# Self and value weights by two levels of Strassen's algorithm as well, in a two-layer graph network

## The chip, the cores and the metric

The kernel runs on one core of a Trainium2 chip. The metric is the time of one execution on the device, in microseconds. Below, PE or TensorE is the matrix engine, DVE or VectorE, ACT or ScalarE, POOL or GpSimd are the other three that compute, and SP issues DMAs.

## The reference

`x` has 128 graphs of 64 nodes with 768 features, `adj` a 64x64 mask for each; all is float32. Two layers, each with a residual and a layer norm:

```python
# layer 0
p     = softmax(h @ h.T / sqrt(768)) * adjacency
attn  = p / (sum(p) + 1e-10)
ctx   = triu(attn, 1) @ (h @ W_left.T + b_left) + diag(attn) * (h @ W_self.T + b_self) \
      + tril(attn, -1) @ (h @ W_right.T + b_right)
x     = layernorm(x + relu(layernorm(ctx) * gamma + beta))
# layer 1, 12 heads of 64
q, k, v = x @ Wq + bq, x @ Wk + bk, x @ Wv + bv
scores  = q @ k.T / 8 + beta * adj, masked where adj is 0
x       = layernorm(x + softmax(scores) @ v)
```

Six weights of 768x768 are applied to all 8192 rows: left, self and right in layer 0, queries, keys and values in layer 1. Everything else is small beside that.

## The kernel before

The rows are taken in 16 blocks of 512 (four tiles of 128 tokens, eight graphs). The input of a block lies turned in SBUF (`hT` for layer 0, `xT` for layer 1: 128 partitions x 6 chunks x 512 tokens). A weight is streamed from DRAM through the pool `wst` (17 buffers of 128x384) for every block.

**Strassen's algorithm, one level.** Weights and inputs are cut in two by two quarters, and seven products replace eight (the variant of Winograd, which shares sums). The sums of weights are formed once at the start and kept in DRAM. The sums of a block's input are formed by GpSimd (`combined`, `combined4`: S1, S2, S4 and an in-place difference, four operations on 128x768). `seven` runs the seven products in the order `ORDER`; each is three matmuls (three chunks of 128 features) into a PSUM bank, for each of two token halves. The variant accumulates in PSUM, so that a bank is read, written on and read again. VectorE empties a bank with one addition (a bias or a partial result). This is how self (`self_part`), values (`values`), and queries and keys (`projected`) are computed, and in blocks 0 to 2 left and right (`side_part`).

**Two levels.** From block 3 on (`DEEP`), left and right are computed together by `both_sides`: each of the seven products, a 256x384 by 384x384 problem, is cut once more. Of the three feature chunks the first two form a 2x2 problem that again takes seven products, and the third is added plainly, two chunks to a product where it fits: the products numbered 2, 5, 4 and 3 take two matmuls, 1, 6 and 7 take one, 11 matmuls for 12. `second_level` forms the sums of one outer factor on GpSimd (four operations: three of 128x128 and one of 128x256). The function `nested` lays the 49 products out: the inner order is 1, 2, 6, 5, 7, 4, 3, and the next outer sum's products 1 and 2 stand ahead of this one's 4 and 3; the outer order is `ORDER2`, 7, 1, 2, 6, 5, 4, 3. What leaves a bank is added into the result in SBUF, and around outer sum 5 GpSimd has twelve additions of result quarters (four into `c21`, four into `c12`, four into `c22`). Each bank's next product waits until VectorE has emptied it. In `both_sides` the left and the right weight stand side by side, so that a matmul has 2 x 192 = 384 columns. The sums of weights for this are made in blocks 0 and 1 by `deepened`: loads by SP, copies and stores by GpSimd's DMA queue, subtractions by VectorE.

**The order of work.** From the line with `manual_schedule` on, every engine runs its instructions in the order in which the code issues them. Around each block the stages follow each other on TensorE: left and right of block n+1, self of block n+1, values of block n, and three rounds of queries and keys of block n. The rest is hung on places of these stages: `at(hooks, place, f)` calls `f` ahead of the product with that number. Left and right have 28 places (`left` 0 to 13, `right` 0 to 13, spread over the 49 products where there are two levels), `own` (self) and `val` (values) 14 each, and each of `qk[0..2]` 14. Between products, `step` takes pieces of work from three queues, `first`, `urgent` and `lazy`. Such pieces are the turns (`turned`: six transposes of 128x512 on VectorE make `hT` or `xT` from a squared layout), the mask of layer 1 (`mask`), the softmax pieces of `scores`, and layer 1's finish (`finish_by_act`: sums of a tile by ScalarE, `mean` on VectorE, sums of squares by ScalarE, `variance` on VectorE, a root, two factors, the normed tiles, four output DMAs on GpSimd's queue). A `GAP` in a queue lets one step pass. In a light step only pieces that are marked run. `settle(key)` issues at once whatever is left of a key.

`weighted(n, hg)` multiplies the softmax of layer 1 with the values for a third of the heads; VectorE divides (`shares`) and GpSimd adds the shares to the residual.

Of the kernel before, what the change touches and what calls it, by code (L numbers as in the profile page):

```python
# [17 lines left out]
P = 128  # L18
# [27 lines left out]
ORDER2 = (7, 1, 2, 6, 5, 4, 3)  # L46
MATRICES = (1, 2, 8, 3, 9, 5, 7, 4, 6)
DEEP = 3


@with_exitstack
def gnn_two_layers(ctx: ExitStack, tc, x, adj, wl, bl, ws, bs, wr, br, gamma, beta,
# [8 lines left out]
    s_p = ctx.enter_context(tc.tile_pool(name="s_p", bufs=1))  # L61
    s2_p = ctx.enter_context(tc.tile_pool(name="s2", bufs=2))
    l0 = ctx.enter_context(tc.tile_pool(name="l0", bufs=1))
    l0t = ctx.enter_context(tc.tile_pool(name="l0t", bufs=T))
    tmp = ctx.enter_context(tc.tile_pool(name="tmp", bufs=2))
    wst = ctx.enter_context(tc.tile_pool(name="wst", bufs=17))
    st = ctx.enter_context(tc.tile_pool(name="st", bufs=2))
# [194 lines left out]
    def deepened(i):  # L262
# [24 lines left out]
        return begin, [(partial(formed, 0),), (partial(formed, 1),), (end, "gap")]  # L287

    def transposed(src, xT, t):

        both = two_banks("ps_x").rearrange("p b (c i) -> p b c i", c=4)
        for c0 in range(0, KC, 3):
            ps = both[:, c0 // 3]
            for c in range(3):
                nc.tensor.transpose(ps[:, c, :], src[:, c0 + c :: KC], ident)
            nc.scalar.copy(xT[:, c0 : c0 + 3, t * P : (t + 1) * P], ps[:, 0:3, :])
# [23 lines left out]

    def combined(xT, n=None):

        a11, a12 = xT[:, 0:HC, 0:HTOK], xT[:, HC:KC, 0:HTOK]
        a21, a22 = xT[:, 0:HC, HTOK:NTOK], xT[:, HC:KC, HTOK:NTOK]
        s1, s2 = (s_p.tile([P, HC, HTOK], F32, tag=f"S{i}", name=f"S{i}") for i in (1, 2))
        nc.gpsimd.tensor_tensor(s1, a21, a22, ALU.add)
        nc.gpsimd.tensor_tensor(a21, a11, a21, ALU.subtract)
        S = {1: a11, 2: a12, 4: a22, 5: s1, 6: s2, 7: a21}
        if n is not None and n >= DEEP:

            S["deep"] = {i: second_level(S[i]) for i in ORDER2[:2]}
        nc.gpsimd.tensor_tensor(s2, s1, a11, ALU.subtract)
        return S
# [94 lines left out]

    def nested(width, sums, load, multiply, view, C, bias0, bias1, hooks):

# [12 lines left out]
        def taken(i, q, ps, dst, add):  # L443
            if add is None:
                nc.scalar.copy(dst, view(ps))
            else:
                nc.vector.tensor_tensor(dst, view(ps), add, ALU.add)  # L447
# [16 lines left out]
        def sub(i, j):  # L464
            for place in range(28):
                if place * 49 // 28 == len(done):
                    for f in hooks.get(place, ()):
                        f()
# [5 lines left out]
            ps = (X if j in (1, 6, 7, 4) else Y)[i][:, 0:width]  # L474
            multiply(F[i], W[i], j, ps)
            if j == 1:
# [10 lines left out]
            elif j == 3:  # L487
                final(i, (0, 1), ps, U[i, 2])

            step(len(done) > 8, j in (5, 1, 4))  # L490

# [101 lines left out]
    def self_part(n, in_sbuf, hooks={}):  # L593

        blk = blocks[n]
        blk["x_all"] = x1_p.tile([P, T, D], F32, tag="x1", name=f"o_{n}")
        o = [blk["x_all"][:, t, :] for t in range(T)]

        def last(t, h, ps, part):
            cols = slice(h * HALF, (h + 1) * HALF)  # L600
            nc.vector.tensor_tensor(o[t][:, cols], ps, bias["s"][:, cols] if part is None else part, ALU.add)

        by_tokens("s", blk["S"], last, in_sbuf, hooks)
        blk["x"] = o

    def side_part(n, nm, in_sbuf, hooks={}):
# [17 lines left out]
    def both_sides(n, hooks):  # L624
# [15 lines left out]

        def multiply(F, w, j, ps):
            f, last = F
            fs = [(f[j], w[j])]
            if j in (2, 5, 4, 3):
                fs.append((last[{2: 1, 5: 2, 4: 2, 3: 3}[j]], w[8 if j in (2, 4) else 9]))
            for k, (a, b) in enumerate(fs):
                nc.tensor.matmul(ps, lhsT=a, rhs=b, start=(k == 0 and j in (1, 2, 5)), stop=(k == len(fs) - 1),  # L647
                                 skip_group_check=True)

        def view(ps):  # L650
# [3 lines left out]
                       for a in range(2) for b in range(2)} for m in range(2) for n_ in range(2)}  # L654
        nested(HALF, sums, load, multiply, view, C,
               lambda b: bias_lr[:, :, b * QUAD : (b + 1) * QUAD],
# [110 lines left out]
    def values(n, hooks={}, in_place=False):  # L767
# [19 lines left out]

        by_tokens("v", blocks[n]["S"], last, None, hooks)
        if not in_place:
# [80 lines left out]
    def weighted(n, hg, halves=(0, 1)):  # L870
# [6 lines left out]
        eT = blk["eT", hg]  # L877
        y = [two_banks(f"ps_y{r}")[:, 0 : len(halves), 0 : 4 * (HD + 1)]
             .rearrange("p h (t c d) -> p h t c d", t=2, c=2) for r in range(2)]
        for k, h in enumerate(halves):  # L880
# [23 lines left out]
    def finish_by_act(n, tiles=range(T), queue=urgent):  # L904
# [34 lines left out]
        def act(f):  # L939
            return f, "act" if queue is urgent else "root"  # L940

        settle(("y", n, 0))
        settle(("y", n, 1))
        later(key, (partial(sums, lambda t, o: nc.scalar.activation(o, xt[t], AF.Identity,  # L944
                                                                    accum_out=total[:, t : t + 1])), "after"),
              GAP, GAP, tiny(mean),
              act(partial(sums, lambda t, o: nc.scalar.activation(o, xt[t], AF.Square, bias=nm[:, t : t + 1],  # L947
                                                                  accum_out=var[:, t : t + 1]))),
              GAP, GAP, tiny(variance), act(root), GAP, tiny(factors),
              *[act(partial(norm, tiles[k : k + 2])) for k in range(0, len(tiles), 2)],  # L950
# [75 lines left out]
    nc.gpsimd.memset(v[:, :, :, :, HD], 1.0)  # L1026

# [3 lines left out]
    for n in range(NBLK):  # L1033
# [12 lines left out]
        for i, (when, hooks, place) in zip(ORDER2, ((0, val, 2), (0, val, 8), (0, qk[0], 8), (0, qk[1], 6),  # L1046
                                                    (0, qk[2], 6), (1, own, 3), (1, val, 3))):
            if when == n:
                begin, steps = deepened(i)
                at(hooks, place, begin)  # L1050
                at(hooks, place + 3, lambda i=i, steps=steps: urgent.extendleft([(("d", i), *f) for f in reversed(steps)]))

        last = n == NBLK - 1
        if p >= 0:
            one = left if not last else qk[0]
            at(one, 2, scores, p, 2, *((1,) if last else (2, None, 4)))
            at(one, 5, weighted, p, 1)
# [3 lines left out]
            elif not last:  # L1061
                at(right, 1, weighted, p, 2)
                at(right, 2, finish_by_act, p)
            else:
                at(qk[1], 5, weighted, p, 2)

        if not last:
            if n > 0:
# [26 lines left out]

                at(own, 3, turn1)

                def sums1():
                    settle(("t1", n))
                    blocks[n]["S"] = combined(blocks[n]["xT"])  # L1100

# [13 lines left out]
                if m == DEEP:  # L1115
                    settle("d")
                if m < DEEP:
                    side_part(m, "l", None, left)
                    side_part(m, "r", None, right)
                    at(own, 0, lambda: nc.vector.tensor_tensor(bias_lr[:, :, HALF:D], bias_lr[:, :, HALF:D],  # L1120
                                                               bias_lr[:, :, 0:HALF], ALU.subtract))
                else:
                    for t, f in enumerate(both_sides(m, {**left, **{2 * len(ORDER) + k: f for k, f in right.items()}})):
                        at(own, 1 + t, f)
# [85 lines left out]
```

## Time and profile before

| | |
|---|---|
| median of 3 runs | 3017.47 us (3014.36 to 3019.05) |
| the profiled execution | 3019.44 us, its span 3017.7 us |
| granted TensorE clock, mean | 0.988 |
| HBM traffic | 539.43 MB read, 77.27 MB written |

One block from the middle, stage by stage, from the stretches of the trace:

| stage | from - to, us | length | PE | DVE | ACT | POOL |
|---|---|---|---|---|---|---|
| left and right of block 9 | 1599.2 - 1660.1 | 60.9 | 57.0 | 34.4 | 21.7 | 34.4 |
| self of block 9 | 1660.1 - 1687.2 | 27.1 | 27.1 | 17.9 | 10.0 | 5.4 |
| values of block 8 | 1687.2 - 1720.9 | 33.7 | 33.7 | 17.9 | 8.1 | 1.8 |
| queries and keys of block 8 | 1720.9 - 1783.3 | 62.4 | 61.9 | 41.7 | 33.1 | 10.5 |

Busy times of an engine are unions of its instructions' spans. A float32 matmul of the program shows as two instructions on PE, each with a weight load on PEld. A span of PE runs on after the next matmul has begun, so the distance between starts tells the rate. The values stage also holds the 16 matmuls of layer 0's context.

### The profile page before, as it was taken

How to read it: one execution, taken by the hardware profiler on the slowest of the kernel's cores; microseconds unless marked ns; L12 is line 12 of the kernel's file. 1: busy time of each engine (PE TensorE's matmuls, PEld its weight loads, DVE VectorE, ACT ScalarE, POOL GpSimd, SP SyncE). 2: the span in 40 equal slices, each digit the busy share in tenths (PEclk: the TensorE clock that was granted, in tenths of full speed). 3: DMA queues.
4: the chain of work that ended last, by engine and by line, in shares of the span. 5: the costliest groups of instructions: out<-in, count | busy, mean ns of one | idle time of the engine just before them, and what ended most of it. 6: DMA issues, size and time to landing. Idle time of an engine off the chain costs nothing.

```text
span 3017.7 us, 49120 instructions
## 1 busy us (share of the span) xinstructions
PE 2907.4 (96%) x17578; PEld 1941.9 (64%) x17578; DVE 1830.7 (61%) x3151; ACT 1129.4 (37%) x2120; POOL 828.0 (27%) x981
## 2 busy tenths in 40 slices
PE   8999999999999999999999999999999999999996
PEld 5557667575675856657575675756758566585684
DVE  5847666565655656556565565656656565566544
ACT  0104324354243443435334343442435424343354
POOL 3132323314042140512405033050331404214011
PEclk9999999999999999999999999999999999999998
DMA  9677876849577586875958668495774967758442
GB/s 317 212 250 254 243 232 193 241 134 279 153 211 222 151 266 151 228 209 170 255 141 263 168 192 242 134 277 156 205 224 140 278 152 229 203 162 257 135 122 77
DMA packets 440273, 613.14 MB, mean 203 GB/s; under 512 B 53584, under 2 KB 416720, under 8 KB 440032
## 3 DMA queue, kind: packets, MB, share of 16 engines
q1 hardware_dynamic: 362096, 493.57, 54.7%
q10 hardware_dynamic: 60848, 44.05, 7.8%
q0 software_dynamic: 17088, 72.37, 6.8%
q8 instruction: 143, 2.34, 0.3%
q14 instruction: 98, 0.80, 0.1%
HBM read 539.43 MB, written 77.27 MB: 204 GB/s over the span
## 4 chain that ended last, share of the span: by engine, by line
PE 77%; ACT 11%; DVE 5%; DMA 5%; issue 1%; POOL 0%; SPq 0%; ACTq 0%; DVEq 0%
PE ps_X L393 30%; PE ps_Y L393 23%; PE ps_Y L647 9%; PE ps_X L647 8%; ACT eT L858 5%; PE ps_ctx L686 3%; ACT unused L947 2%; PE sc L841 2%; DMA wlr<-lr_d 2%; ACT unused L944 2%; PE u L536 1%; ACT uqk L810 1%; PE ps_y L887 1%; DMA sq<-x1d 1%; ACT L858 1%
## 5 line engine op out<-in xcount | busy, mean ns | idle before, releaser
L900 POOL TENSOR_TENSOR o<-o,shares 128x512 f32<-128x512 f32 (+1 forms) x102 | 126.4, 1248 | 1388.6 <-DVE shares L896 1309.7
L393 PE MATMUL ps_X<-xT,wqk 128*128 128x256 f32 x1728 | 396.9, 381 | 9.1 <-ACT uqk L810 9.1
L393 PEld LDWEIGHTS ps_X<-xT,wqk 128*128 128x128 f32 x1728 | 325.7, 190 | 67.8 <-ACT uqk L810 21.6
L858 ACT ACTIVATE eT<-s 32x256 f32<-32x256 f32 x768 | 317.8, 414 | 48.3 <-DVE s L866 37.6
L393 PE MATMUL ps_Y<-S,wqk 128*128 128x256 f32 x1152 | 264.3, 379 | 0.0
L691 ACT ACTIVATE unused<-o 128x768 f32<-128x768 f32 x60 | 50.6, 843 | 507.0 <-DVE o L689 264.9
L393 PEld LDWEIGHTS ps_Y<-S,wqk 128*128 128x128 f32 x1152 | 218.9, 190 | 29.8
L447 DVE TENSOR_TENSOR lr<-ps_Y,u_deep 128x384 f32<-128x384 f32 x273 | 152.1, 557 | 140.1 <-PE ps_Y L647 116.9
L647 PE MATMUL ps_Y<-wlr,q 128*128 128x384 f32 x546 | 208.6, 491 | 0.0
L810 ACT ACTIVATE uqk<-ps_X,bq 128x256 f32<-128x256 f32 x144 | 68.3, 474 | 361.6 <-PE ps_X L393 360.8
L647 PE MATMUL ps_X<-wlr,q 128*128 128x384 f32 x364 | 153.9, 505 | 48.7 <-DVE u_deep L447 33.2
L393 PE MATMUL ps_X<-wv,xT 128*128 128x384 f32 x576 | 195.3, 489 | 0.0
L818 DVE TENSOR_TENSOR q<-ps_Y,uqk 128x256 f32<-128x256 f32 x144 | 61.0, 424 | 203.7 <-ACT uqk L810 119.7
L393 PE MATMUL ps_X<-ws,hT 128*128 128x384 f32 x540 | 179.9, 486 | 3.4 <-DVE u L424 3.4
L944 ACT ACTIVATE unused<-o 128x768 f32<-128x768 f32 x62 | 52.3, 843 | 288.2 <-POOL o L900 164.6
L393 PEld LDWEIGHTS ps_X<-wv,xT 128*128 128x128 f32 x576 | 108.0, 190 | 80.3 <-issue 8.4
L447 DVE TENSOR_TENSOR u_deep<-ps_X,lr 128x384 f32<-128x384 f32 x195 | 107.3, 550 | 82.6 <-PE ps_X L647 80.3
L393 PEld LDWEIGHTS ps_X<-ws,hT 128*128 128x128 f32 x540 | 102.2, 190 | 74.4 <-DVE u L424 4.3
L647 PEld LDWEIGHTS ps_Y<-wlr,q 128*128 128x128 f32 x546 | 100.5, 190 | 68.3 <-DVE lr L447 4.5
L647 PEld LDWEIGHTS ps_X<-wlr,q 128*128 128x128 f32 x364 | 64.0, 190 | 115.8 <-DVE u_deep L447 41.2
L393 PE MATMUL ps_X<-S,wqk 128*128 128x256 f32 x576 | 138.2, 385 | 0.0
L393 PE MATMUL ps_Y<-xT,wqk 128*128 128x256 f32 x576 | 135.6, 385 | 0.0
(248 smaller groups left out, 5461.6 us busy)
## 6 DMA issues: line engine op xcount, KB each, us to landing
wlr<-lr_d SPq DMA_DIRECT2D x819, 192.0 KB, 4.1
wqk<-qk_d SPq DMA_DIRECT2D x672, 192.0 KB, 2.4
wv<-d_v SPq DMA_DIRECT2D x192, 192.0 KB, 4.4
ws<-d_s SPq DMA_DIRECT2D x180, 192.0 KB, 4.8
wv<-in_L_gnn_Wv_dram SPq DMA_DIRECT2D x144, 192.0 KB, 2.5
ws<-in_L_gnn_W_self_dram SPq DMA_DIRECT2D x135, 192.0 KB, 3.7
xa<-in_x_dram SPq DMA_DIRECT2D x64, 384.0 KB, 6.0
out_dram<-o POOLq DMA_DIRECT2D x62, 384.0 KB, 5.0
```

Source lines behind the costliest of these rows:

```text
L393: nc.tensor.matmul(ps, lhsT=a, rhs=b, start=(c == 0 and i in (1, 2, 5)), stop=(c == len(fs) - 1), skip_group_check=True)
L447: nc.vector.tensor_tensor(dst, view(ps), add, ALU.add)
L647: nc.tensor.matmul(ps, lhsT=a, rhs=b, start=(k == 0 and j in (1, 2, 5)), stop=(k == len(fs) - 1), skip_group_check=True)
L686: nc.tensor.matmul(ps[g * L : (g + 1) * L, h, :], lhsT=blk["aT"][:, t, g * L : (g + 1) * L], rhs=blk["lr"][t][:, g, cols], start=True, sto ...
L691: nc.scalar.activation(unused(), o[t], AF.Identity, accum_out=total[:, t : t + 1])
L810: nc.scalar.activation(u, ps, AF.Identity, bias=bias["qk"[j]][:, c : c + 1])
L818: nc.vector.tensor_tensor(dst, ps, part, ALU.add)
L841: nc.tensor.matmul(sc[g * L : (g + 1) * L, r, t, c, :], lhsT=q[rows, c, tok], rhs=k[rows, c, tok], start=True, stop=True)
L858: nc.scalar.activation(e[cols, :, rows], pairs[rows, :, cols], AF.Exp)
L900: nc.gpsimd.tensor_tensor(res, res, shares.rearrange("p h (t c) d -> p (h t) c d", c=2), ALU.add)
L944: later(key, (partial(sums, lambda t, o: nc.scalar.activation(o, xt[t], AF.Identity, accum_out=total[:, t : t + 1])), "after"), GAP, GAP, ...
L947: act(partial(sums, lambda t, o: nc.scalar.activation(o, xt[t], AF.Square, bias=nm[:, t : t + 1], accum_out=var[:, t : t + 1]))),
```

## The change

Self from block 3 on, and values for blocks 3 to 14, go through `nested` too. One weight alone gives matmuls of 192 columns: 77 for 42 of 384. Their weight sums are made in blocks 1 and 2 by the new `deepened_alone` (fourteen calls: two tiles loaded, five pieces copied and four stored by GpSimd's queue, four subtractions on VectorE) and are loaded as pairs (`PAIRS`), five transfers for each of the seven outer sums. In this form `nested` has 14 places, ScalarE empties no bank, and all steps but those after product 7 are light. The second-level sums of the first two outer sums are formed ahead: for self at `right` 12, for values in `combined`.

Layer 1's turns (`turn1`) go from `own` 3 to `right` 7, the third weighted sum from `right` 1 to `left` 12, its finish from `right` 2 to `right` 0, with five `GAP`s instead of two ahead of `mean` and of `variance`. `wst` has 14 buffers instead of 17, the pool of second-level sums 3 instead of 2.

```diff
+PAIRS = ((1, 2), (8, 6), (5, 9), (7, 4), (3,))
-    s2_p = ctx.enter_context(tc.tile_pool(name="s2", bufs=2))
+    s2_p = ctx.enter_context(tc.tile_pool(name="s2", bufs=3))
-    wst = ctx.enter_context(tc.tile_pool(name="wst", bufs=17))
+    wst = ctx.enter_context(tc.tile_pool(name="wst", bufs=14))
...
+    deep_d = {nm: tc.dram_tile([7, len(PAIRS), P, 2, QUAD], F32, name=f"deep_{nm}") for nm in "sv"}
+    def deepened_alone(nm, i):
+        src, w = pieces[nm][i], {}
+        place = {m: deep_d[nm][i - 1, k, :, j, :] for k, pair in enumerate(PAIRS) for j, m in enumerate(pair)}
+        def half(k, h):
+            if nm == "s":
+                return src[:, k, h * QUAD : (h + 1) * QUAD]
+            return src[:, k, :].rearrange("p (j r d) -> p r j d", r=2, d=HD)[:, h]
...
+        def begin():
+            for k in range(2):
+                w[k] = wst.tile([P, 2, QUAD], F32, tag="w", name="w_deep")
+                for h in range(2):
+                    nc.sync.dma_start(out=shaped(w[k][:, h, :]), in_=half(k, h))
+            for m, k, h in ((1, 0, 0), (2, 1, 0), (8, 2, 0), (3, 1, 1), (9, 2, 1)):
+                nc.gpsimd.dma_start(out=shaped(place[m]), in_=half(k, h))
+        def formed():
+            b11, b12, b21, b22 = (w[k][:, h, :] for k in range(2) for h in range(2))
+            for out, a, b in ((b11, b12, b11), (b12, b22, b12), (b22, b22, b11), (b21, b21, b22)):
+                nc.vector.tensor_tensor(out, a, b, ALU.subtract)
+        def end():
+            for m, k, h in ((5, 0, 0), (7, 0, 1), (4, 1, 0), (6, 1, 1)):
+                nc.gpsimd.dma_start(out=place[m], in_=w[k][:, h, :])
...
-            S["deep"] = {i: second_level(S[i]) for i in ORDER2[:2]}
+            S["alone" if values else "deep"] = {i: second_level(S[i]) for i in ORDER2[:2]}
...
-            if add is None:
+            if add is None and places == 28:
                 nc.scalar.copy(dst, view(ps))
+            elif add is None:
+                nc.vector.tensor_copy(dst, view(ps))
...
-            step(len(done) > 8, j in (5, 1, 4))
+            step(places == 14 or len(done) > 8, j in (5, 1, 4) if places == 28 else j != 7)
...
+    def alone(nm, S, view, C, bias0, bias1, hooks):
+        def load(i):
+            w = {}
+            for k, pair in enumerate(PAIRS):
+                two = wst.tile([P, 2, QUAD], F32, tag="w", name=f"w{nm}")
+                nc.sync.dma_start(out=two[:, 0 : len(pair), :], in_=deep_d[nm][i - 1, k, :, 0 : len(pair), :])
+                w.update({m: two[:, j, :] for j, m in enumerate(pair)})
+            return w
+        def sums(i):
+            return S.get("alone", {}).get(i) or second_level(S[i])
+        nested(QUAD, sums, load, view, C, bias0, bias1, hooks, 14)
...
-        by_tokens("v", blocks[n]["S"], last, None, hooks)
+        if n < DEEP or in_place:
+            by_tokens("v", blocks[n]["S"], last, None, hooks)
+        else:
...
+            alone("v", blocks[n]["S"], lambda ps: ps[:, 0:QUAD].rearrange("p (j d) -> p j d", d=HD), C,
+                  lambda k: b0[:, k], lambda k: b1[:, k], hooks)
...
+        wait = [GAP] * (5 if queue is urgent and len(tiles) == T else 2)
...
-              GAP, GAP, tiny(mean),
+              *wait, tiny(mean),
...
-              GAP, GAP, tiny(variance), act(root), GAP, tiny(factors),
+              *wait, tiny(variance), act(root), GAP, tiny(factors),
...
+        for nm, when in (("s", ((1, left, 1), (1, left, 6), (1, left, 11), (1, right, 5), (1, right, 10), (1, val, 8),
+                                (1, qk[0], 6))),
+                         ("v", ((2, left, 3), (2, left, 9), (2, right, 3), (2, right, 9), (2, own, 2), (2, own, 7),
+                                (2, val, 5)))):
...
-            at(one, 2, scores, p, 2, *((1,) if last else (2, None, 4)))
+            at(one, 2, scores, p, 2, *((1,) if last else (2, None, 2)))
...
-                at(right, 1, weighted, p, 2)
-                at(right, 2, finish_by_act, p)
+                at(left, 12, weighted, p, 2)
+                at(right, 0, finish_by_act, p)
...
-                at(own, 3, turn1)
+                at(*((own, 3) if n < 2 else (right, 7)), turn1)
...
-                    blocks[n]["S"] = combined(blocks[n]["xT"])
+                    blocks[n]["S"] = combined(blocks[n]["xT"], n, True)
...
+                    def sums_self():
+                        S = blocks[m]["S"]
+                        S["alone"] = {i: second_level(S[i]) for i in ORDER2[:2]}
+                    at(right, 12, sums_self)
```

## The prediction

> **What bounds the kernel now.** I read the page's busy shares first, then a table of one steady block by stage (left and right, self, values, queries and keys), then the timelines of TensorE, VectorE and GpSimd in it, and last the groups by shape for prices.
>
> ```profile
> PE 2907.4 (96%) x17578; PEld 1941.9 (64%) x17578; DVE 1830.7 (61%) x3151; ACT 1129.4 (37%) x2120; POOL 828.0 (27%) x981
> ```
>
> TensorE is the bound on the average. The stages differ, though. In this table the columns are stretch, its length, then busy time of PE, PEld, DVE, ACT, POOL, then granted clock, DMA share and GB/s:
>
> ```profile
> 1599.20:1660.10 60.90, 56.98 (x351) 32.80 (x351) 34.44 (x64) 21.66 (x42) 34.41 (x46) 0.97 0.97 295
> 1660.10:1687.20 27.10, 27.10 (x85) 15.96 (x84) 17.85 (x23) 9.97 (x12) 5.42 (x3) 1.00 0.71 198
> 1687.20:1720.90 33.70, 33.70 (x118) 17.59 (x117) 17.85 (x26) 8.06 (x17) 1.81 (x1) 1.00 0.60 155
> 1720.90:1783.30 62.40, 61.93 (x542) 53.33 (x541) 41.65 (x76) 33.09 (x64) 10.52 (x13) 1.00 0.48 137
> ```
>
> The second and third rows are the self and value stages, which the change rewrites: TensorE never pauses there, GpSimd works 5.4 and 1.8 us, VectorE two thirds and half of the time. Only the first row, the stage that already has two levels, has pauses:
>
> ```profile
> 1539.42 2.75 PE L393 MATMUL ps_Y<-xT,wqk 128*128 128x256 f32 x12
> 1656.65 0.60 PE L587 MATMUL ps_a<-ident,a 128*128 128x128 f32 x4
> 1664.02 4.03 PE L393 MATMUL ps_Y<-ws,hT 128*128 128x384 f32 x12
> 1642.38 0.88 PE L647 MATMUL ps_X<-wlr,q 128*128 128x384 f32 x2 [0.89 <-POOL lr L461]
> 1647.11 1.34 PE L647 MATMUL ps_X<-wlr,q 128*128 128x384 f32 x2 [2.56 <-DVE u_deep L447]
> ```
>
> ```profile
> 1640.78 1.04 DVE L919 TENSOR_SCALAR f<-f 128x4 f32<-128x4 f32 x1 [2.62 <-ACT unused L944]
> 1646.10 0.50 DVE L922 TENSOR_SCALAR f<-f 128x4 f32<-128x4 f32 x1 [2.23 <-ACT unused L947]
> ```
>
> Both pauses (0.89 and 2.56 us) begin where VectorE stands in its queue behind `mean` and `variance` of layer 1's finish, which wait for ScalarE's sums, while PSUM waits to be emptied. After the second one the clock is granted at half for 3.41 us in 11 of these 13 stages, which is another 1.7 us.
>
> **Products.** A matmul runs as two passes. Twelve passes of 384 columns take 4.03 us, the last one 0.486 of it, so 0.322 apart; of 256 columns 0.216; of 128 (the four transposes) 0.109. That is a straight line, 0.162 at 192 columns. A self or value stage had 42 products of 2 x 0.322 (27.05, as the table shows); it gets 77 of 2 x 0.162, 24.9: **-2.1 us** in 13 self stages (block 3 on) and 12 value stages (blocks 3 to 14).
>
> One rule speaks against this: the Trainium skill, "TensorE: Matmul & The Clock Gate", Part 3, says that a weight load overlaps running matmuls only if it goes to another row group. Here every load covers all rows, and yet 384-column passes stand 0.322 apart, their column time alone, and each of the transposes' 128x128 loads fits into 0.109. The trace disagrees, so I count loads at nothing. By the rule, with the 0.109 added to each pass, the 35 extra products would make a stage 5.5 us longer, not 2.1 shorter.
>
> **VectorE.** Prices:
>
> ```profile
> L447 DVE TENSOR_TENSOR lr<-ps_Y,u_deep 128x384 f32<-128x384 f32 x273 | 152.1, 557 | 140.1 <-PE ps_Y L647 116.9 <-ACT u_deep L445 17.2 <-DVE u_deep L447 0.5
> L818 DVE TENSOR_TENSOR q<-ps_Y,uqk 128x256 f32<-128x256 f32 x144 | 61.0, 424 | 203.7 <-ACT uqk L810 119.7 <-PE ps_Y L393 82.0 <-issue 0.5
> L785 DVE TENSOR_TENSOR v<-ps_Y,u 64x192 f32<-64x192 f32 x24 | 8.5, 356 | 9.4 <-PE ps_Y L393 9.1
> L314 DVE STREAM_TRANSPOSE xT<-sq 128x512 f32<-128x512 f32 x84 | 88.5, 1078 | 0.0
> ```
>
> An eviction of 192 columns costs 0.36 (the line through 384 and 256, and the row of 64x192). A stage had 14 x 0.557 = 7.8 us of them and gets 49 x 0.36 = 17.6. In the order of the built program each of the seven outer sums takes 11 products (3.56 us), and VectorE does in it: two evictions of product 7, one queued piece, then the next sum's 1 and 2, this sum's 4 and 3, the next sum's 6. TensorE may not start 6 before 1 is evicted, nor 7 before 6 is. Without a queued piece this fits. With a turn of 1.08 in it: product 7's drain 0.53, 0.36 + 0.40, 1.08, 0.36 + 0.40, twice 0.29 (evictions that need not wait start 0.07 before the one ahead ends), then 6's eviction, and the next 7 comes 3.98 after the last: **+0.42** each. Four of layer 1's turns stay in the self stage, since moving them to left and right gets only two done before its end: +1.7. In the value stage two of layer 0's turns fall into the last sums: +0.8. Bounds: 0 (PSUM's two banks absorb it) and 1.08 each.
>
> **GpSimd.** Prices:
>
> ```profile
> L345 POOL TENSOR_TENSOR q<-hT 128x128 f32<-128x128 f32 x52 | 23.7, 457 | 1.0
> L347 POOL TENSOR_TENSOR q<-hT 128x256 f32<-128x256 f32 x52 | 38.1, 733 | 0.0
> L462 POOL TENSOR_TENSOR lr<-lr,lr 128x384 f32<-128x384 f32 x52 | 51.9, 997 | 4.1
> L326 POOL TENSOR_TENSOR S<-xT 128x768 f32<-128x768 f32 x16 | 28.9, 1808 | 385.0 <-DVE xT L314 336.8 <-ACT xT L296 48.2
> ```
>
> Each stage gets second-level sums of seven outer sums (3 x 0.457 + 0.733 = 2.1 each) and, around outer sum 5, twelve additions of 192 columns, 0.59 each between 0.457 and 0.733. They stand in one queue: from the first eviction of sum 5 come 12 x 0.59 and the sums for 4 and 3, 11.3 us, and product 6 of sum 3 needs the last of these. TensorE has 26 products until there, 8.4 us. GpSimd starts 1.4 later than that count, two turns give back 0.8: **a wait of 3.4 us** in each self and value stage. In left and right the same queue is 12 x 1.0 + 4.2 = 16.2 against 26 x 0.644 = 16.7, which is why it hardly shows today. Bounds: 2.0 (additions at 0.457) and 5.0 (at 0.733).
>
> After it, the last sum has no next sum's products between 7 and 4, so 7's eviction lies open: +0.6 in each stage. At the end of self GpSimd still owes two outer sums (1.8 each) and a second level (2.1) before the values' first product 6: 5.7 against 11 products and that 0.6, 4.2: +1.5. The gap of 3.4 is longer than the one that halves the clock now, so 1.7 x 11/13 = 1.4 follows it; in self this runs beside the 1.5, I count 1.6 for the two, in values it counts whole.
>
> Self: -2.1 + 1.7 + 3.4 + 0.6 + 1.6 = **+5.2**. Values: -2.1 + 0.8 + 3.4 + 0.6 + 1.4 = **+4.1**.
>
> **Left and right.** The finish now waits five places for its sums instead of two, and starts earlier, since the third weighted sum moves from `right` 1 to `left` 12. Counting products in the new order, the variance stands where ScalarE has been done for about 0.4 us, and `mean` still waits 1.6 us but nothing on TensorE needs the evictions behind it. So 0.89 + 2.56 + 1.4 of clock go. What is late next is GpSimd: its two additions of weighted shares and the sums for 5 come just ahead of the chain above, which ends 0.9 after TensorE would want it. **-4.0** in 13 stages; bounds -4.9 and 0. The two second-level sums added at `right` 12 stand between the four output DMAs (0.55 each) on GpSimd's queue and end over 2 us before the self stage asks for them.
>
> **Once only.** Fourteen weights are deepened in blocks 1 and 2: 126 DMAs on GpSimd at 0.73 (the row of `lr_d`) and 56 subtractions at 0.405. Three double ones in block 0's last stage cost 63.0 against 62.4. So 3 us if it stays hidden, 30 if GpSimd, at 34 of 61 us in left and right, is overrun; I take 8. At nothing I count ScalarE (its work stays), queries and keys (two more turns at their start, against 20 us of idle VectorE; uncovered 2 x 1.08 a block), and the subtractions for `more_v` and the bias. SP gets 35 loads a stage for 21, priced as a rival.
>
> **Sum.** 13 x 5.2 + 12 x 4.1 - 13 x 4.0 + 8 = +73. The profiled execution took 3019.4 (span 3017.7), 2 above the median of the three runs; so 3092 profiled, **3090** as a median. This likeliest case by itself: 3045 to 3125.
>
> **Rivals.** *GpSimd is not late, faster.* If the twelve additions cost 0.35 or less, or their results are needed later than I read, 3.4 and what follows it vanish: self +0.2, values -0.7, left and right -4.9, sum -62, 2955. It is faster already where self and values together lose less than 3.5 us a block (52 - 8 over 12.5). For it: GpSimd is busy 27% on the page. Against: four shapes lie on one line with a fixed 0.19 us each. 0.2.
> *DMA becomes the bound, slower still.* Self asks 6.2 MB in 24.9 us, 249 GB/s, and left and right now run at a share of 0.97 with 295; the pool has 14 buffers for 17, 2.4 us less lead, where the shortest lead of a landed tile there is 3.35. Two microseconds in 13 blocks: 3116. Against: in self GpSimd stretches the stage to 30 us, 206 GB/s. 0.1.
> *Left and right keep their pause* because another wait (GpSimd, DMA) takes its place: +52, 3140. 0.08.
> *The forecast*: 0.62.
>
> About 0.2% (6 us) is what a measurement of this kernel can tell. Faster 0.2 (the first rival), same 0.04 (the forecast's low end), slower 0.76. The range of 2990 to 3130 takes in the likeliest case's bounds, most of the DMA case, and the near half of the way to the first rival.
>
> **What would show it.** Right: TensorE pauses of about 3 us before product 6 of the third sum in self and values, ended by GpSimd, half clock behind them; GpSimd near 29 us of work issued in self; left and right at 57. Wrong: self at 27 or less; passes of 192 columns further apart than 0.17; a wait for `deep_s` or `deep_v` on TensorE; GpSimd additions under 0.4 us.

## The result, and the profile after

The changed kernel takes 3194.18 us (median of 4 runs, 3190.79 to 3201.07) against 3016.72 for the kernel before on the same chip: ratio 1.0591, 95% interval 1.0572 to 1.0611. The sign of the forecast was right and its size was not: +177 us where +73 was predicted, outside the range.

Busy shares of the changed kernel (page, part 1):

```profile
PE 2950.4 (92%) x19328; PEld 2196.6 (69%) x19328; DVE 2018.5 (63%) x4084; ACT 1127.8 (35%) x2120; POOL 1416.4 (44%) x2107
```

TensorE fell from 96% to 92%, GpSimd rose from 27% to 44%. A steady block by stage (left and right, self, values, queries and keys; columns as in the prediction's table):

```profile
1123.50:1181.20 57.70, 55.30 (x352) 32.13 (x351) 34.75 (x65) 21.66 (x42) 38.10 (x54) 1.00 0.99 287
1181.20:1219.90 38.70, 31.53 (x156) 27.91 (x155) 22.54 (x57) 9.96 (x12) 20.62 (x35) 0.87 0.82 241
1219.90:1255.40 35.50, 33.16 (x188) 26.56 (x188) 24.43 (x59) 8.06 (x17) 23.97 (x42) 1.00 0.63 188
1255.40:1317.90 62.50, 61.97 (x542) 53.37 (x542) 43.05 (x79) 32.88 (x64) 10.55 (x13) 1.00 0.49 140
```

The second row has taken the damage: self has 7.2 us without a matmul, and its clock is granted at 0.87. The pauses in it, on TensorE's timeline (start, span, engine, line, what; idle time before and what ended it):

```profile
1183.39 0.56 PE L473 MATMUL ps_X<-ws,q 128*128 128x192 f32 x2 [1.10 <-DVE u_deep L494]
1188.03 0.98 PE L473 MATMUL ps_X<-ws,q 128*128 128x192 f32 x2 [3.42 <-issue]
1214.99 0.59 PE L473 MATMUL ps_X<-ws,q 128*128 128x192 f32 x2 [1.81 <-POOL q L383]
1217.15 1.65 PE L473 MATMUL ps_X<-ws,S 128*128 128x192 f32 x4 [0.45 <-DVE u_deep L496]
```

The third is the pause that was predicted, before product 6 of outer sum 3 (the last in the order) and ended by GpSimd. The first two, 2 and 7 us into the stage, were not. The first is a turn of layer 1 that stands on VectorE ahead of the stage's first eviction. For the second, "issue" names no releaser; VectorE's timeline shows both, and GpSimd's what was behind the second:

```profile
1181.90 1.11 DVE L351 STREAM_TRANSPOSE xT<-sq 128x512 f32<-128x512 f32 x1
1187.30 0.36 DVE L496 TENSOR_TENSOR o<-ps_Y,u_deep 128x192 f32<-128x192 f32 x1 [4.06 <-ACT lr L725]
```

```profile
1174.64 1.08 POOL L1010 DMA_DIRECT2D out_dram<-o  x2
1175.74 0.47 POOL L382 TENSOR_TENSOR q<-hT 128x128 f32<-128x128 f32 x1
...
1179.44 0.46 POOL L385 TENSOR_TENSOR q<-hT,q 128x128 f32<-128x128 f32 x1
1179.84 1.09 POOL L1010 DMA_DIRECT2D out_dram<-o  x2
```

The eviction at 1187.30 is the first of the stage that writes `o`, the output tile of this block. Its pool `x1_p` has two buffers, and this one is still being read by the stores of an earlier block's output. The second pair was issued at 1179.84 to 1180.93, behind self's two new second-level sums, and the page gives a store 6.4 us to landing (median):

```profile
out_dram<-o POOLq DMA_DIRECT2D x62, 384.0 KB, 6.4
```

By the landing times in the trace the last of them landed at 1187.09. In 11 of the 12 steady self stages this first eviction starts 0.22 us after the last store has landed. Before, the same tile was first written 6.1 us into the stage, which began at 1660.10; with 192-column products it is wanted at about 2:

```profile
1666.21 0.56 DVE L601 TENSOR_TENSOR o<-ps_Y,u 128x384 f32<-128x384 f32 x1 [1.44 <-ACT lr L664]
```

The group of these evictions names the stores and ScalarE's swap as releasers (the idle time of all of them, in us, and what ended it), so this was a theory that needed a test:

```profile
L496 DVE TENSOR_TENSOR o<-ps_Y,u_deep 128x192 f32<-128x192 f32 x273 | 96.9, 355 | 87.6 <-DMA out_dram<-o 31.6 <-ACT lr L725 24.3 <-PE ps_Y L473 15.7
```

Mean lengths of the stages (blocks 4 to 15 for left and right and self, blocks 3 to 14 for values) and of the two stages in which weights are deepened, in us. They come from one traced run of each kernel, whose own time stands beside the median:

| kernel | median | traced run | left and right | self | values | left and right, self of block 2 | of block 3 |
|---|---|---|---|---|---|---|---|
| before | 3016.7 | 3019.4 | 60.65 | 27.10 | 33.60 | 62.9, 27.1 | 60.9, 27.1 |
| changed | 3194.2 | 3194.9 | 57.31 | 38.70 | 35.69 | 67.2, 36.6 | 77.5, 51.9 |
| lr_alone | 2957.2 | 2954.8 | 55.82 | 27.10 | 33.60 | 58.9, 32.3 | 55.4, 27.1 |
| lr_14 | 2993.9 | 3002.1 | 58.48 | 27.43 | 33.60 | 58.9, 36.8 | 60.4, 27.1 |
| self_old | 3034.7 | 3034.5 | 57.58 | 28.20 | 35.59 | 58.9, 35.0 | 76.7, 30.6 |
| values_old | 3125.3 | 3128.0 | 57.57 | 37.81 | 33.61 | 68.4, 34.6 | 56.6, 37.6 |
| sums_later | 3150.8 | 3162.1 | 57.93 | 35.05 | 35.87 | 68.6, 38.5 | 78.5, 48.5 |
| stores_by_act | 3205.3 | 3211.4 | 58.24 | 38.58 | 35.59 | 67.8, 39.8 | 77.5, 50.1 |
| stores_other | 3130.0 | 3141.6 | 58.28 | 33.38 | 35.74 | 67.0, 38.5 | 76.1, 48.7 |
| bias_by_vector | 3141.1 | 3137.3 | 58.12 | 33.52 | 35.52 | 67.0, 35.9 | 77.6, 47.8 |
| turns1_by_act | 3124.2 | 3124.6 | 58.08 | 32.64 | 35.57 | 68.2, 38.1 | 78.3, 44.0 |
| turns0_by_act | 3110.7 | 3107.8 | 57.90 | 34.02 | 33.42 | 66.3, 33.4 | 75.9, 47.6 |
| deepen_spread | 3170.8 | 3172.2 | 58.69 | 38.46 | 35.51 | 58.9, 34.8 | 65.7, 38.2 |
| all_three | 3109.3 | 3109.4 | 58.65 | 33.93 | 35.54 | 58.9, 33.7 | 65.7, 32.6 |

From the first two rows: self 13 x 11.6 = +151, values 12 x 2.1 = +25, left and right 13 x -3.34 = -43; what blocks 2 and 3 take beyond that is 13.8 + 33.1 = +47; first and last stages -4. The sum is 176; the spans differ by 175.4. A traced run lies up to 12 us from its median (sums_later, stores_other, lr_14), so a difference of under 1 us a stage between two kernels is not told by one trace.

### The profile page after: what moved, and what is told of

The parts are those of the page before. It is cut to its first block, busy times and chain, and to the rows that moved or that the text cites. A ratio compares the mean times of both kernels' runs of the same rounds, so it can differ in the third digit from the quotient of the medians.

```text
span 3193.1 us, 56413 instructions
## 1 busy us (share of the span) xinstructions
PE 2950.4 (92%) x19328; PEld 2196.6 (69%) x19328; DVE 2018.5 (63%) x4084; ACT 1127.8 (35%) x2120; POOL 1416.4 (44%) x2107
## 4 chain that ended last, share of the span: by engine, by line
PE 64%; POOL 9%; DMA 9%; ACT 7%; DVE 7%; issue 3%; SPq 0%; DVEq 0%; ACTq 0%; POOLq 0%
PE ps_Y L473 16%; PE ps_X L430 15%; PE ps_X L473 15%; PE ps_Y L430 12%; ACT eT L927 5%; DMA wlr<-lr_d 4%; PE ps_ctx L747 3%; PE sc L910 2%; DMA sq<-x1d 2%; PE u L584 1%; ACT uqk L879 1%; PE ps_y L960 1%; DVE u_deep L496 1%; POOL v L511 1%; POOL v L510 1%
## 5 line engine op out<-in xcount | busy, mean ns | idle before, releaser
L473 PE MATMUL ps_X<-ws,q 128*128 128x192 f32 x364 | 109.4, 384 | 98.5 <-issue 43.0
L496 DVE TENSOR_TENSOR o<-ps_Y,u_deep 128x192 f32<-128x192 f32 x273 | 96.9, 355 | 87.6 <-DMA out_dram<-o 31.6
L473 PEld LDWEIGHTS ps_X<-ws,q 128*128 128x128 f32 x364 | 58.7, 200 | 133.8 <-issue 61.7
L473 PEld LDWEIGHTS ps_Y<-wlr,q 128*128 128x128 f32 x546 | 102.4, 191 | 68.6 <-issue 2.0
L473 PE MATMUL ps_X<-wlr,hT 128*128 128x384 f32 x312 | 122.0, 501 | 16.0 <-DMA wlr<-lr_d 16.0
L473 PE MATMUL ps_Y<-ws,q 128*128 128x192 f32 x546 | 130.0, 350 | 0.2 <-DVE o L496 0.2
```

## The experiments

**Left and right alone**, on the kernel before:

```diff
+        wait = [GAP] * (5 if queue is urgent and len(tiles) == T else 2)
-              GAP, GAP, tiny(mean),
+              *wait, tiny(mean),
...
-              GAP, GAP, tiny(variance), act(root), GAP, tiny(factors),
+              *wait, tiny(variance), act(root), GAP, tiny(factors),
-            at(one, 2, scores, p, 2, *((1,) if last else (2, None, 4)))
+            at(one, 2, scores, p, 2, *((1,) if last else (2, None, 2)))
-                at(right, 1, weighted, p, 2)
-                at(right, 2, finish_by_act, p)
+                at(left, 12, weighted, p, 2)
+                at(right, 0, finish_by_act, p)
```

> The kernel before with only the later finish (five gaps), the third weighted sum at left 12 and the finish at right 0: no second level in self or values, layer 1's turns where they were. If left and right's two pauses are freed by these moves by themselves: -2.5 to -4 us in each of 13 stages, 2965 to 2985 us. If the gain needs the turns at right 7 too, or if the later stores of the output hold up the next self stage as they seem to in the changed kernel: 3010 to 3040.

2957.24 us, ratio to before 0.9794 (0.9776 to 0.9812): below the range. One steady block, left and right and self, and the only pause in that stage:

```profile
1031.40:1087.00 55.60, 55.02 (x352) 32.15 (x351) 34.52 (x64) 21.67 (x42) 34.14 (x46) 1.00 0.98 292
1087.00:1114.10 27.10, 27.10 (x86) 15.97 (x85) 17.84 (x23) 9.97 (x12) 5.43 (x3) 1.00 0.88 266
```

```profile
1084.30 1.56 PE L647 MATMUL ps_X<-wlr,S 128*128 128x384 f32 x4 [0.21 <-DVE u_deep L447]
```

Both pauses and the half clock after them are gone. This part of the change is a gain of 63 us by itself, and this kernel is the best of all that ran.

**The same with 14 buffers for weights:**

```diff
-    wst = ctx.enter_context(tc.tile_pool(name="wst", bufs=17))
+    wst = ctx.enter_context(tc.tile_pool(name="wst", bufs=14))
```

> lr_alone with 14 weight buffers instead of 17. Theory A (left and right gained 5.5 us alone and 2.5 in the changed kernel because the weights have 14 buffers and land later): 1.5 to 3 us more in each of 13 stages, 2975 to 2995 against 2957. Rival (the difference is GpSimd's two more second-level sums and layer 1's turns at right 7): 2950 to 2965.

2993.86 us, 36.6 more, in theory A's range. Left and right lose 2.7 us of the 4.8 they had gained, to a wait for weights, which the changed kernel has as well (second row, from block 8's left and right there):

```profile
1091.44 1.62 PE L647 MATMUL ps_X<-wlr,hT 128*128 128x384 f32 x2 [4.02 <-DMA wlr<-lr_d]
```

```profile
1552.69 0.89 PE L473 MATMUL ps_X<-wlr,hT 128*128 128x384 f32 x2 [1.82 <-DMA wlr<-lr_d]
```

So most of what left and right gave up in the changed kernel (57.31 for 55.82) is the price of three buffers. That they are 1.2 us better there than here (58.48) with as many buffers says little: kernels that share the changed one's left and right run from 57.3 to 58.7.

**One part undone each.** First self by one level (`self_part` always takes `by_tokens`, nothing is deepened for it), then values likewise:

```diff
-        if n < DEEP:
+        if True:
             by_tokens("s", blk["S"], last, in_sbuf, hooks)
-                    at(right, 12, sums_self)
```

> The changed kernel with self weights by one level in all blocks; values keep two levels. Self stages back at 27 us in 13 blocks (-11.7 each, 152 us), and what deepening self's weights cost in block 2 and the crowded first deep self stage go (another 20 to 30): 3005 to 3025 us. If the idle time only moves into left and right or values: above 3060.

3034.74 us (10 runs, 3016.72 to 3045.21): 159 less than the changed kernel, and 10 above the range that was expected. Self explains most of it, 12 x 10.5 + 21.3 in block 3; values keep their 35.6, so nothing moved over to them. Self is back at 28.2 and not at 27, which makes about the 10.

```diff
-        if n < DEEP or in_place:
+        if True:
             by_tokens("v", blocks[n]["S"], last, None, hooks)
```

> The changed kernel with values by one level in all blocks; self keeps two levels. Values back at 33.6 (-1.9 in 12 blocks, 23 us), and the deepening of values' weights in the stages of block 3 gone (lr 77.5 to about 58, self 51.9 to about 39: 30 us): 3130 to 3150. If once-only work is cheap, as the prediction had it: 3165 to 3175.

3125.26 us, 69 less and 5 below the expected range: 25 in the value stages, 35 in block 3 (77.5 + 51.9 to 56.6 + 37.6), 11 in self. All of block 3's extra time hung on deepening the weights of values.

**What holds the start of self.** The two sums one place later, so that the stores come first on GpSimd:

```diff
-                    at(right, 12, sums_self)
+                    at(right, 13, sums_self)
```

> The changed kernel with the two second-level sums for self one place later, so that GpSimd issues the second pair of output stores ahead of them, some 3 us earlier; no other engine's order differs. Theory A (the first finished eviction of the self stage writes the tile that these stores still read): 3.4 to 4.5 us of TensorE's idle time at the start of self and the half clock behind it go, but for about 0.8 us; 5.5 to 7 us less in each of 13 self stages, 3105 to 3125 us. Theory B (that eviction waits for ScalarE's swaps of left and right, which the trace names) or C (the first weights of self land late): no change, 3185 to 3200.

3150.84 us, 43 less; about half of what theory A asked for, nothing that B or C allow. The last store now goes out 4.3 us ahead of the self stage (it begins at 1369.8) instead of 0.8, and the eviction still waits for it, now under its own name (GpSimd's, then VectorE's timeline):

```profile
1365.46 0.54 POOL L1010 DMA_DIRECT2D out_dram<-o  x1 [0.38 <-ACT o L1006]
```

```profile
1373.80 0.36 DVE L496 TENSOR_TENSOR o<-ps_Y,u_deep 128x192 f32<-128x192 f32 x1 [1.95 <-DMA out_dram<-o]
```

This store took 8.1 us to land, at 1373.58; a likely reason, not tested, is that self's weights were being loaded beside it. To take the rest, the stores were given to ScalarE, which makes the data:

```diff
-                nc.gpsimd.dma_start(out=out_t[n, t], in_=xt[t])
+                (nc.scalar if queue is urgent else nc.gpsimd).dma_start(out=out_t[n, t], in_=xt[t])
```

> sums_later with the output stores of the urgent finish issued from ScalarE's queue, behind the norms that make them, and not from GpSimd's. Theory A (the rest of the wait at the start of self, 1.3 to 1.8 us with half clock after it in some stages, is still the landing of these stores, which GpSimd issues up to 1 us after the norms): 1.5 to 3 us less in each of 13 stages, 3110 to 3130 against 3151. Rival (the stores land as late from any queue, since the DMA engines are full of weights at that time): within 8 us of 3151.

3205.32 us, 54 worse than sums_later. Both theories missed, but the hold is seen again. On ScalarE's timeline and then VectorE's:

```profile
1384.29 1.93 ACT L1006 ACTIVATE o<-o,f,f 128x768 f32<-128x768 f32 x2
1386.96 4.44 ACTq L1010 DMA_DIRECT2D out_dram<-o  x3
1391.68 0.83 ACT L723 COPY swap<-lr 64x768 f32<-64x768 f32 x1 [5.47 <-DVE lr L496]
```

```profile
1396.36 0.36 DVE L496 TENSOR_TENSOR o<-ps_Y,u_deep 128x192 f32<-128x192 f32 x1 [3.46 <-ACT lr L724]
```

The norms were done at 1386.2, but three issues stretch to 1391.40; the last of these stores landed at 1396.08, 0.28 us before the eviction, and the trace again names a swap. What held the issues apart is in the trace's semaphores: ahead of each of these issues ScalarE's queue waits for a semaphore, the one that its own landing will count on, and on this a load of SyncE's was still under way. The three waits ended at 1386.88, 1389.86 and 1390.98, the times at which an input tile and two pieces of self's weights landed. GpSimd's four stores in the changed kernel, 1174.64 to 1180.93, have no such wait. The Trainium skill, "DMA: Bandwidth & Descriptors", section "Issuing engine by pattern", says the queues of SyncE and ScalarE are generally faster than GpSimd's: for the landing this agrees (median 5.1 us against 7.3 in sums_later), for the whole way from the norm to free memory it does not.

The proof is the changed kernel with stores of the same size, issued at the same times, from a tile that nobody waits for (the kernel leaves out the output of these blocks):

```diff
-                nc.gpsimd.dma_start(out=out_t[n, t], in_=xt[t])
+                nc.gpsimd.dma_start(out=out_t[n, t], in_=affine_of["gamma"] if queue is urgent
+                                    and n >= DEEP - 1 and n < NBLK - 2 else xt[t])
```

> The changed kernel, but in 12 blocks the output stores of the finish read a constant tile (gamma) and not the output tile: the same stores at the same places with the same bytes, and the next self stage's tile is no longer held by them (the output of these blocks is wrong). Theory A (the hold is what costs, not the traffic): idle time of 3.4 us and half clock of 3.4 us go in 12 stages, 3100 to 3125 against 3194. Rival (the stores' traffic delays self's weights, and a wait for those takes the place): 3140 to 3180.

3129.97 us, 64 less, 5 above theory A's range and clear of the rival's. Self goes from 38.70 to 33.38 with the swaps and the traffic in place:

```profile
1367.15 0.36 DVE L496 TENSOR_TENSOR o<-ps_Y,u_deep 128x192 f32<-128x192 f32 x1 [0.48 <-ACT lr L724]
```

In the changed kernel the first eviction into `o` comes 5.9 to 7.2 us into the steady self stages, here at 2.2 to 2.6, although the stores still go out and land when they did. So the hold of the tile was shown to cost 5.3 us a stage, half clock included.

**What else self and values wait for.** Part of GpSimd's work given to VectorE, on sums_later:

```diff
-                nc.gpsimd.tensor_tensor(c12[q], c12[q], bias1(q[1]), ALU.add)
+                (nc.vector if places == 14 else nc.gpsimd).tensor_tensor(c12[q], c12[q], bias1(q[1]), ALU.add)
```

> sums_later with the four additions of bias1 around outer sum 5 in self and values done by VectorE instead of GpSimd: 2.4 us off the queue that product 6 of outer sum 3 waits for, 4 x 0.36 more on VectorE. Theory A (that queue is what is late in both stages): the wait of 1.8 us, the 0.45 behind it and the half clock go, -3 in self and -2 in values, less a little for VectorE: 3080 to 3105 against 3151. Rival (VectorE is the bound of these sums and the wait only changes its releaser): 3140 to 3165.

3141.11 us, only 10 less, in the rival's range; the two kernels' intervals against before overlap (1.0387 to 1.0425 and 1.0413 to 1.0466), so that even the 10 is hardly shown. Next to nothing comes from values, and the 1.5 us a stage in self is in part that the traced run of sums_later is 11 us above its median. GpSimd's 1.81 is gone and other waits, as long in all, stand in its place (self, then values):

```profile
1384.27 0.56 PE L473 MATMUL ps_X<-ws,q 128*128 128x192 f32 x2 [0.55 <-POOL o L511]
1387.76 0.56 PE L473 MATMUL ps_X<-ws,q 128*128 128x192 f32 x2 [0.66 <-DVE u_deep L496]
1389.72 0.59 PE L473 MATMUL ps_X<-ws,q 128*128 128x192 f32 x2 [0.67 <-DVE u_deep L496]
...
1420.32 0.56 PE L473 MATMUL ps_X<-wv,q 128*128 128x192 f32 x2 [0.55 <-POOL v L511]
1423.65 0.56 PE L473 MATMUL ps_X<-wv,q 128*128 128x192 f32 x2 [0.49 <-DVE u_deep L496]
```

Then VectorE was relieved as well: on bias_by_vector, the turns of one layer done as plain copies on ScalarE (the kernel leaves out the turning). The edit for layer 1; for layer 0 the key is "t", from block 5 on:

```diff
         def turn(c):
+            if key[0] == "t1" and key[1] >= 2:
+                nc.scalar.copy(xT[:, c, :].rearrange("p (s j) -> p s j", j=Q), sq[:, :, c::KC])
+                return
```

> bias_by_vector with layer 1's six turns of each block from the third on done as plain copies by ScalarE instead of transpositions by VectorE (the data are not turned, so the output is wrong): 4 to 5 x 1.08 us less on VectorE in the self stage, ScalarE has 28 us idle there. Theory A (VectorE's queue is what self's sums still wait for: 0.42 a turn, and 1.09 where one stands ahead of the first eviction of self): -2 to -3.5 us in each of 13 stages, 3095 to 3115 against 3141. Rival (the chain of evictions itself, or GpSimd, sets the pace): within 10 us of 3141.

> bias_by_vector with layer 0's turns, which stand in the value stage's last sums and at the queries' start, done as plain copies by ScalarE from the deep value stages on (output wrong). Theory A (VectorE is what is late in values too, at 0.4 us a turn and more where bias1's additions stand beside it): value stages 35.5 to about 34, 3115 to 3130 against 3141. Rival (VectorE is not the bound there): within 8 us of 3141.

3124.15 us for layer 1's turns, 17 less, between the theories: self -0.9 a stage, and -3.8 in block 3. With a turn less ahead of it VectorE came sooner to the hold of the tile, and waits there longer:

```profile
1731.35 0.36 DVE L499 TENSOR_TENSOR o<-ps_Y,u_deep 128x192 f32<-128x192 f32 x1 [2.96 <-DMA out_dram<-o]
```

3110.70 us for layer 0's, 30 less, a little beyond theory A: values fall by 2.1 to 33.42, just under the one-level stage's 33.60:

```profile
1386.00:1419.40 33.40, 32.65 (x187) 26.82 (x188) 21.92 (x59) 12.12 (x21) 22.45 (x38) 1.00 0.76 216
```

So with GpSimd relieved VectorE was what was late in values: the turns gave 2.1. Taking work from GpSimd and giving it to VectorE had given nothing. Whether the turns alone would have been enough was not run.

**The weights deepened elsewhere**, on the changed kernel:

```diff
-        for nm, when in (("s", ((1, left, 1), (1, left, 6), (1, left, 11), (1, right, 5), (1, right, 10), (1, val, 8),
-                                (1, qk[0], 6))),
-                         ("v", ((2, left, 3), (2, left, 9), (2, right, 3), (2, right, 9), (2, own, 2), (2, own, 7),
-                                (2, val, 5)))):
+        for nm, when in tuple((nm, tuple((k, hooks, place) for hooks, place in
+                                     ((val, 8), (qk[0], 3), (qk[0], 8), (qk[1], 2), (qk[1], 6), (qk[1], 10), (qk[2], 3))))
+                         for nm, k in (("s", 1), ("v", 2))):
```

> The changed kernel with the deepening of the fourteen weights moved to value, query and key stages of the same two blocks, where GpSimd works less than a third of the time. Theory A (the once-only cost of some 45 us is GpSimd's queue in left and right and self of blocks 2 and 3): 25 to 40 us less, 3155 to 3170 against 3194. Rival (it is the traffic of DMA, wherever it stands, or it comes back in the queries' stages): less than 12 us.

3170.82 us, 23 less, just short of theory A. What the queue looked like in the changed kernel's block 3, whose self stage begins at 587.7 (GpSimd, then TensorE, then VectorE):

```profile
573.57 2.21 POOL L322 DMA_DIRECT2D deep_v<-w_deep  x4
579.96 3.66 POOL L313 DMA_DIRECT2D deep_v<-d_v  x5
583.61 1.66 POOL L322 DMA_DIRECT2D deep_v<-w_deep  x3
586.39 0.54 POOL L322 DMA_DIRECT2D deep_v<-w_deep  x1 [1.11 <-DMA deep_v<-d_v]
591.34 2.17 POOL L1010 DMA_DIRECT2D out_dram<-o  x4
```

```profile
578.86 1.65 PE L473 MATMUL ps_X<-wlr,q 128*128 128x384 f32 x2 [5.13 <-POOL q L383]
600.21 0.98 PE L473 MATMUL ps_X<-ws,q 128*128 128x192 f32 x2 [9.53 <-POOL q L385]
```

```profile
599.48 0.36 DVE L496 TENSOR_TENSOR o<-ps_Y,u_deep 128x192 f32<-128x192 f32 x1 [10.17 <-DMA out_dram<-o]
```

The four DMAs at 573.57 stand ahead of a second-level sum, and TensorE waits 5.13 us for it. The nine from 579.96 on stand, with self's two second-level sums, ahead of the four output stores, which go out at 591.34 although the norms were done at 585.87. So the wait of 9.53 us is the hold of the output tile again, longer than elsewhere: VectorE stands 10.17 us before its first eviction into `o`, and TensorE goes on 0.7 us after that one has begun. The trace puts TensorE's wait down to a second-level sum (L385), which had ended at 599.26.

In deepen_spread the 5.13 is gone and VectorE's wait at the start of that stage is back at 4.08 us; what is left is the landing of weights, in block 3's left and right and in the next one, which takes 67.8 us for 57.4:

```profile
714.11 2.95 PE L473 MATMUL ps_Y<-wlr,hT 128*128 128x384 f32 x4 [5.97 <-DMA wlr<-lr_d]
```

**All three repairs together** (sums_later, bias_by_vector, deepen_spread):

> The changed kernel with the three repairs that gained something, together: self's two second-level sums behind the second pair of stores, bias1 added by VectorE, the weights deepened in value, query and key stages. If the gains add up (43, 10 and 23 us): 3105 to 3130. Two levels in self and values would still be over 100 us behind left and right's part alone with the same 14 buffers (2994).

3109.27 us, ratio to before 1.0298 (1.0256 to 1.034): the gains add up, 85 us of the 177. It is still 115 behind lr_14, which has the same 14 buffers and one level in self and values.

## Why the prediction was right or wrong

**The sign** came out for the reason given: products got 2.1 us shorter a stage, and the other engines could not keep up. The waits it announced are there, at their places, and the kernel is slower without the largest cost too, which was not on the list (stores_other, 3130).

**Products: right.** Four passes of 192 columns take 0.65 us (0.162 each) wherever nothing waits. The rule it was weighed against (the Trainium skill, "TensorE: Matmul & The Clock Gate", Part 3), would have made each stage 5.5 us longer by itself; turns0_by_act shows a two-level value stage at 33.4 against 33.6, so the measurement decides against it. The rule is one line of that part, which a few lines earlier also lets a load that goes to the background weight buffer run ahead; with that the rows here agree, though no run shows which buffer a load goes to. Only behind a pause is a load seen: the second pass of the product that ends it starts 0.237 after the first, not 0.162.

**The step that failed** is the one sentence on the sums at `right` 12: they "stand between the four output DMAs (0.55 each) on GpSimd's queue and end over 2 us before the self stage asks for them", at nothing. It followed the sums to their reader and not the stores behind them to theirs. These stores free the tile that self evicts into. The stage wants it 4 us earlier than before (2.2 for 6.1 us into it), and the last store goes out later: 4.8 to 6.5 us ahead of the stage before, 3.5 to 4.3 in lr_alone with the five gaps, at most 0.8 behind the two sums. Priced by stores_other: 64 us of the 104 that were missing.

**Once only: the term was mis-sized.** I took 8 and gave 30 as the bound; blocks 2 and 3 took 47 more. Of these, the 9.5 in block 2's self have nothing to do with deepening: lr_14, which deepens nothing new, has 36.8 there too, with the same hold (VectorE waits 9.75 us for the stores). Deepening itself is nearer 41: 8.3 in block 2's left and right (67.2, and 58.9 in self_old) and 33 in block 3. The bound asked whether GpSimd had time in the stage as a whole; what counted was which work stood behind its DMAs, a second-level sum once and the output stores once, so that some 6 us of block 3's are the hold again. deepen_spread gets 23 back, and values_old shows that the 33 of block 3 go with the value weights.

**Third-sum wait: right place, too long.** 1.81 + 0.45 instead of 3.4 + 0.6. Product 6 was released by the second of the four operations of a second-level sum (L383), not by the last, which is 1.2 us earlier. The half clock behind it, counted in 11 of 13, came in five of the 12 steady self stages and in one value stage. The 1.5 at the end of self came as 1.06, in seven of the 12. In six of the 12 the trace names a wait for `deep_v` for the 1.81, which the prediction had as a sign of being wrong; the pause is as long where it names GpSimd, and bias_by_vector took it away by relieving GpSimd's queue. GpSimd was busy 20.6 us in self, where near 29 was named as a sign of being right. Also, the terms of VectorE and GpSimd in values were added, 0.8 + 3.4; bias_by_vector shows that they do not add: with the one gone the other took as long. Values: +2.1 for +4.1, which hides 24 us of what was missing: luck.

**VectorE in self**: 1.7 predicted for four turns; taking all away gave 0.9, but with the hold still in the stage, so its size there stays open. One turn, ahead of the first eviction, cost 1.10 at a place that the sum did not have. With the hold gone self is at 33.38, +6.3 where the terms without it made +5.2.

**Left and right**: -4.0 predicted, -4.8 alone with 17 buffers, -3.3 in the changed kernel. GpSimd was not 0.9 late. What took its place was the weights, the "DMA becomes the bound" rival, with the right cause (14 buffers) and put in the wrong stage: priced at 26 us in self, measured at 37 by lr_14, most of it in left and right. In the changed kernel left and right give up 1.5 us a stage to it.

**The other rivals.** "GpSimd is not late" fell with the 1.81. "Left and right keep their pause" came true in part, as just said.

**The range** missed because its upper end was built from the bounds of terms that were on the list; the largest cost was not on it. The 104 us add up but for rounding: 13 x 5.3 = 69 for the hold, 13 x 1.1 = 14 for the rest of self, 39 once only, 13 x 0.7 = 9 in left and right, -24 in values and -4 in the first and last stages.

## What to carry to other kernels

When a stage is made faster at its front, list every buffer that its first results go into and who still reads it: the deadline of the old readers moves forward by as much as the first result does. A step put into a queue delays everything behind it, so follow each of these, DMA stores too, to whoever waits for its end. And split a change that comes as a bundle: here 63 us of gain from a few moved places were buried under 240 us of cost from the rest.

## What was not expected of the hardware

- Two pauses of about 1.10 and 3.1 to 4.5 us within 6 us were followed by 6.83 us of half clock in 9 of the 12 steady self stages and 3.41 in the other three; the 2.56 us pause of before by 3.41 in 11 of 13 stages, and the pauses of 1.81 and 0.45 us at the end of self by 3.41 or 6.83 in five of 12. In the whole execution the mean granted clock fell from 0.988 to 0.971 (2.9% of 3193 is 93 us of clock not granted, against 36 before), and was 0.993 in lr_alone.
- A store of 384 KB takes 0.545 us to issue on GpSimd and 0.35 on ScalarE, but in stores_by_act the last three issues of one block stood 1 to 3 us apart (1386.96 to 1391.06), each behind a wait for a load of SyncE's to land, and so the faster queue was the later one.
- Stores that are issued earlier do not land by as much earlier: in sums_later the last store of a block goes out 3.5 us sooner (4.3 us ahead of the stage, not 0.8), and lands some 2 us sooner (3.3 to 4.3 us into the stage in most blocks, 5.6 to 6.9 in the changed kernel).
